# A two-layer graph transformer on one core: q of the second block, two row sums and the last feed-forward weights are placed elsewhere

## The chip, the core and the metric

The kernel runs on one core of one Trainium2 chip. The metric is the device time of one execution in microseconds (us), and the profile is one execution taken by the hardware profiler. Engines are named as in the profile: PE (matrix multiply), DVE (vector), ACT (scalar), POOL (GpSimd) and SP (the engine that only issues transfers here). ACT, SP and POOL each have a queue of their own for issuing DMA transfers. An instruction on an engine runs after the one ahead of it in that engine's order.

## The reference

Two layers of graph attention over N = 2708 nodes with 512 features, 8 heads of 64, and a feed-forward part of width 2048, all in float32. One layer, cut to what matters:

```python
mask = adj.astype(jnp.float32) + jnp.eye(n, dtype=jnp.float32)
q = (h @ Wq.T + bq).reshape(n, N_HEADS, D_K)
k = (h @ Wk.T + bk).reshape(n, N_HEADS, D_K)
v = (h @ Wv.T + bv).reshape(n, N_HEADS, D_K)
scores = jnp.einsum('nhd,mhd->hnm', q, k) / jnp.sqrt(jnp.float32(D_K))
scores = jnp.where(mask[None, :, :] == 0, jnp.float32(-1000000000.0), scores)
attn = jax.nn.softmax(scores, axis=-1)
ctx = jnp.einsum('hnm,mhd->nhd', attn, v).reshape(n, D_MODEL)
attn_out = ctx @ Wo.T + bo
h1 = _layer_norm(h + attn_out, ln1_g, ln1_b)
ff = jax.nn.relu(h1 @ W1.T + b1) @ W2.T + b2
h2 = _layer_norm(h1 + ff, ln2_g, ln2_b)
```

The adjacency matrix is sparse: a node has a handful of neighbours (22 at most are planned for), so attention only has to look at a short list for each node.

## The kernel before

**Lists and ranks.** `first` walks over the 22 tiles of 128 nodes (the last tile has 20) and makes k and v of layer 0 for each (line 835 and 841 on PE), which go to a table in memory, `kv_d`. Beside that, `lists` turns the rows of the adjacency matrix into lists of neighbours, `counted` counts them, and `ranked` (line 735) sorts all nodes by the length of their lists: two pairs of matmuls, a few DVE operations ending in `ranks` (line 764), 22 scatters by POOL to a table `rec_d` (line 768), and a load of the sorted lists back (line 779). From then on "tile g" means 128 nodes of the sorted order, tile 0 those with the longest lists and tile 21 the 20 with the shortest. `ident_i` (line 794) holds which node stands where, and a gather by it (`gather`, line 951) fetches rows of a table for one sorted tile. In layer 0, q and the rows of x are in the nodes' old order, so a sorted tile's q has to be gathered from `q_d`, and only after all of `q_d` has been written.

**Queries.** `first_queries` makes q of layer 0 for all 22 old tiles (t = 0 to 21, line 882), writing them to `q_d` in pairs through `written` (line 868). So that attention can begin ahead of the end of that, the q of some sorted tiles is made a second time from gathered rows of x: `own_rows` gathers x, `turned_own` transposes it on PE (tile `zT`, line 1100 and 1102), and `own_query` multiplies by Wq again (lines 922 and 923). At t = OWN = 9 this is done for the first block, tiles 21 and 20, whose q stays in a buffer; two steps on, for the second block, tiles 19 and 18, whose q goes out to a table `q_own` and comes back through SP when `asked` for it (line 971). `listed`, which turns the sorted lists into indices, stands at t = 8.

**Attention.** `attend` is a generator of steps. A step handles two list slots of one tile: POOL gathers the k and v rows of 128 neighbours for each slot (line 952, five `kv` buffers, asked for at least three chunks ahead), `weights` multiplies by q and sums over each head on DVE (lines 991 and 997), and a step later `weigh` takes exponents on ACT (line 1010), scales one slot's v on ACT (line 1017, eight operations) and the other on DVE (line 1023), and adds (line 1030). Two steps after a tile's last slot come `sums`, and three steps after it `divided`, which writes the finished tile `cx` on ACT (line 1061). The tiles are taken in the order 21, 20, 19, 18, 8, 9, 7, 10, ..., with planned list lengths (`CAPS`) of 3, 5, 6, 7, 10 and 9 slots for the first six. `advance` spends credit on steps and stops when two finished tiles wait; `through(k)` steps until block k is finished. The q of the next tile is asked for on the second step of a tile.

**Feed-forward.** The sorted tiles are taken in 11 blocks of two: (21, 20), (19, 18), (8, 9), ... `attended` transposes the block's `cx`, gathers x (`xb`), multiplies by Wo (`o`), adds and normalises (`h`; the square root of each normalisation is `rd` on POOL, line 1090). `turned` transposes `h` to `hT`. `feed_forward` runs 16 steps f: `pf` (line 1265, from `hT` and W1), `ft` on ACT (line 1273), and the products `a` with W2 three steps behind (line 1253). Within these steps `advance` puts attention of the next blocks: in block 0 with 1.1 credit up to f = 9, and at f = 10 the next block's `attended` begins.

**Weights.** W1 and W2 come in eight parts each (`load_w1`, `load_w2`), parts 0 and 1 during the last steps of `first`, parts 2 to 4 on ACT's queue during the first three steps of the queries, and parts 5 to 7 on SP's queue after all queries, since their places in memory hold the x and q tiles of the query stage until then. `load_second` (line 1137) loads rows of shift vectors and adds two pairs of them on DVE (`ln_b`, line 1144) inside `first`.

**Order.** PE, ACT and SP run in the order in which the program is written. DVE is so in the query stage, and POOL in `first` and `first_queries`; elsewhere the order on these two is set by a scheduler when the kernel is built, which may place an instruction of a later part ahead.

Of the kernel before, what the change touches and what calls it, by code (L numbers as in the profile page):

```python
# [18 lines left out]
P = 128  # L19
# [26 lines left out]
OWN = 9  # L46
# [424 lines left out]
def by_edges(ctx: ExitStack, tc: tile.TileContext, x, xT, adj, layers, out, good):  # L471
# [49 lines left out]
    q_own = dram.tile([N, DM], F32, name="q_own")  # L521
# [340 lines left out]
    def first_queries(bq, wq, listed, pa, tokens, meanwhile):  # L862
# [15 lines left out]
        for t in range(NT):  # L878
            r = size(t)
            if t % 2 == 0 and made:  # L880
                written()
            q = project(tokens(t, 1), r, wq, "q", other=t % 2 > 0)
            if t % 2 == 0:
                qs = wts.tile([P, 2, DM], F32, tag=f"w2_{5 + t // 2 % 3}", name="qs")
                made.append((t, qs))
            nc.vector.scalar_tensor_tensor(
                qs[:r, t % 2], q[:r], DK**-0.5, bq[:r], ALU.mult, ALU.add
            )
            if t == OWN - 1:
                listed()  # L890
                pa.__exit__(None, None, None)
                at = ctx.enter_context(tc.tile_pool(name="at", bufs=2))
                for g in blocks[0]:
                    own[g] = at.tile([P, DM], F32, tag="q", name="q", bufs=QB)
                to = dict(own)
                next(ahead)
            if t in (OWN, OWN + 2):
                k = (t - OWN) // 2
                zTs = [turned_own(g, xr) for g, xr in zip(blocks[k], xrs)]
                for g, xr, zT in zip(blocks[k], xrs, zTs):  # L900
                    own_query(g, zT, to.get(g, xr), bq, wq)
                    advance(0.5)
                xrs = [own_rows(g) for g in blocks[1]] if k == 0 else []
            meanwhile(t)
# [14 lines left out]
    def own_query(g, zT, to, bq, wq):  # L919

        r = size(g)
        q = project(lambda c: zT[:, c, :r], r, wq, "q")
        nc.vector.scalar_tensor_tensor(to[:r], q[:r], DK**-0.5, bq[:r], ALU.mult, ALU.add)
        if g in blocks[1]:
            nc.sync.dma_start(out=q_own[g * P : g * P + r, :], in_=to[:r])
# [35 lines left out]
    def asked(n, g):  # L961
# [5 lines left out]
        if n == 0 and g not in blocks[1]:  # L967
            gather(q[:r], q_d[0], ident_i[:r, g : g + 1])
        else:
            table = q_own if n == 0 else q_d[n]  # L970
            nc.sync.dma_start(out=q[:r], in_=table[g * P : g * P + r, :])
# [137 lines left out]
    class Layer:  # L1109
# [27 lines left out]
        def load_second(self, part, temp):  # L1137
# [3 lines left out]
            def sum_of(one, tag, other):  # L1141
                t, u = row(w, one, tag), temp()
                nc.sync.dma_start(out=u, in_=other.to_broadcast([P, DM]))
                nc.vector.tensor_tensor(t, t, u, ALU.add)
# [200 lines left out]
    def attend(n, got):  # L1345
# [15 lines left out]
        for k, step in enumerate(steps):  # L1361
            if step:
                g, s0, c, i, last = step
                if i == 0:
                    t = Tile(g, q)
# [3 lines left out]
                if i == 1 and g != order[-1]:  # L1369
                    q = asked(n, order[order.index(g) + 1])  # L1370
# [35 lines left out]
    early = {}  # L1406

    def beside_keys(t):
# [3 lines left out]
        if t > NT - 3:  # L1412
            now.load_second(t + 2 - NT, temp)
# [3 lines left out]
    def beside_queries(t):  # L1417

        if len(now.w2) < 5:
            now.load_w1(len(now.w1), nc.scalar)  # L1420
            now.load_w2(len(now.w2), nc.scalar)
        if t > OWN:
            advance(1.0 if t < NT - 7 else 0.45)
        if t == NT - 7:
# [3 lines left out]
        if t == NT - 6:  # L1428
# [10 lines left out]
    for j in range(len(now.w1), NFC // 2):  # L1439
        now.load_w1(j)  # L1440
        now.load_w2(j)
    behind, pool = None, []
    for n in range(NL):
# [26 lines left out]
        turning = projecting = None  # L1470
        for k, block in enumerate(blocks):
# [4 lines left out]
            for f, zs in enumerate(now.feed_forward(block, hs, hT)):  # L1476
# [8 lines left out]
                if more and f == 10:  # L1485
# [29 lines left out]
                if not last and not more:  # L1515
# [90 lines left out]
```

## Time and profile before

| what | value |
|---|---|
| time, median of 3 runs | 1980.74 us (1980.46 to 1982.29) |
| the profiled execution | 1984.12 us, of which the span of the trace is 1982.0 us |
| DVE busy | 1303.1 us (66%) |
| ACT busy | 934.6 us (47%) |
| POOL busy | 798.3 us (40%) |
| k and v stage ends, queries begin | 172.2 us |
| feed-forward of block 0 begins | 290.4 us |
| feed-forward of block 1 begins | 358.3 us |
| layer 1's first queries | about 1160 us |

Times within the trace are counted from the start of the span. An idle time of PE is shown with the instruction that released it, so that "PE waits for ft" means that PE's next multiply needed a tile that ACT wrote late. A line number belongs to the instruction, not to the place that called for it: all gathers by POOL are line 952, and only the tile's name tells which they are.

### The profile page before, as it was taken

What the parts mean: (1) busy time and instruction counts of PE and PEld (TensorE: products, weight loads), DVE (VectorE), ACT (ScalarE), POOL (GpSimd) and SP (SyncE); (2) the same over time, 40 slices, a digit from 0 to 9 for tenths busy, and PEclk for the clock granted to TensorE, in tenths of its full rate; (3) what the DMA queues carried; (4) which work ended last, traced back from release to release, by engine and by line L of the source; (5) the groups of instructions that cost most, each with busy time, mean ns of one, the idle gap of its engine ahead of it and who ended that gap; (6) DMA issues with size and microseconds to landing.
All of it is one profiled execution on the core that took longest, in us unless ns stands there. A gap on an engine that the chain in (4) does not pass through costs nothing. (4 is left out here: it accounts for less than half of the span.)

```text
span 1982.0 us, 20873 instructions
## 1 busy us (share of the span) xinstructions
PE 1903.5 (96%) x6162; PEld 1104.5 (56%) x6162; DVE 1303.1 (66%) x2140; ACT 934.6 (47%) x3219; POOL 798.3 (40%) x708
## 2 busy tenths in 40 slices
PE   8999888999999999999999997999999999999997
PEld 3443344565656556566566643556666566666664
DVE  6884478675957969568442025888587989777421
ACT  4660235464545646447441112665446765655320
POOL 3104436362634636435210023455356655544210
PEclk9999899999999999999999998999999999999998
DMA  8988658464745747455310746756465766554100
GB/s 321 357 296 293 191 200 296 154 208 143 227 154 174 236 150 246 154 173 176 133 58 22 225 157 225 258 182 212 155 208 186 244 205 225 177 188 151 42 11 13
DMA packets 131518, 367.96 MB, mean 186 GB/s; under 512 B 16701, under 2 KB 36525, under 8 KB 128687
## 3 DMA queue, kind: packets, MB, share of 16 engines
q0 software_dynamic: 69104, 246.35, 37.6%
q1 hardware_dynamic: 55780, 103.86, 15.3%
q10 hardware_dynamic: 6510, 16.34, 2.2%
q8 instruction: 50, 0.82, 0.2%
q14 instruction: 74, 0.60, 0.1%
HBM read 315.14 MB, written 51.35 MB: 185 GB/s over the span
## 5 line engine op out<-in xcount | busy, mean ns | idle before, releaser
L952 POOL DMA_INDIRECT kv<-kv_d,idx x420 | 547.0, 1302 | 494.0 <-DVE acc L1030 337.2
L1253 PE MATMUL a<-w,ft 128*128 128x512 f32 (+1 forms) x1408 | 665.3, 597 | 9.5 <-ACT ft L1273 9.5
L1265 PE MATMUL pf<-hT,w 128*128 128x256 f32 (+1 forms) x2816 | 638.2, 374 | 15.8 <-ACT ft L1273 8.0
L1265 PEld LDWEIGHTS pf<-hT,w 128*128 128x128 f32 x2816 | 523.2, 192 | 193.4 <-issue 107.7
L1253 PEld LDWEIGHTS a<-w,ft 128*128 128x128 f32 (+1 forms) x1408 | 255.9, 186 | 234.1 <-issue 198.3
L1273 ACT ACTIVATE ft<-pf,b 128x256 f32<-128x256 f32 (+1 forms) x352 | 157.9, 458 | 424.4 <-PE pf L1265 424.1
L991 DVE TENSOR_TENSOR kv<-kv,q 128x1024 f32<-128x1024 f32 (+3 forms) x222 | 256.5, 1158 | 144.6 <-DMA kv<-kv_d,idx 122.0
L1017 ACT ACTIVATE kv<-kv,p 128x64 f32<-128x64 f32 x1232 | 311.0, 335 | 5.0
L997 DVE TENSOR_REDUCE sc<-kv 128x16 f32<-128x1024 f32 (+3 forms) x222 | 254.6, 1153 | 1.0
L1030 DVE TENSOR_TENSOR acc<-acc,kv 128x1024 f32<-128x1024 f32 (+2 forms) x178 | 203.8, 1145 | 35.9 <-ACT kv L1017 35.4
L1090 POOL TENSOR_TENSOR rd<-va,mhalf 128x1 f32<-128x1 f32 (+1 forms) x88 | 85.7, 974 | 270.0 <-DVE va L1088 268.6
L1010 ACT ACTIVATE p<-sc,minus 128x8 f32<-128x8 f32 (+1 forms) x420 | 103.3, 295 | 190.3 <-DVE sc L997 189.9
L1023 DVE TENSOR_TENSOR kv<-kv,p 128x512 f32<-128x512 f32 (+1 forms) x178 | 121.5, 683 | 69.5 <-ACT p L1010 69.5
L568 PE MATMUL o<-wo,cT 128*128 128x512 f32 (+1 forms) x352 | 155.1, 593 | 0.5 <-ACT cT L1105 0.5
L568 PEld LDWEIGHTS o<-wo,cT 128*128 128x128 f32 (+1 forms) x352 | 65.1, 186 | 86.5 <-issue 75.8
L1061 ACT ACTIVATE cx<-acc,su 128x64 f32<-128x64 f32 (+1 forms) x352 | 88.5, 333 | 42.4 <-DVE su L1053 34.9
L1285 DVE TENSOR_TENSOR h<-a,h 128x512 f32<-128x512 f32 (+1 forms) x44 | 29.7, 677 | 106.0 <-PE a L1253 105.9
L1094 DVE SCALAR_TENSOR_TENSOR h<-h,rd,ln_b 128x512 f32<-128x512 f32 (+1 forms) x88 | 65.8, 748 | 48.1 <-POOL rd L1090 48.1
L660 ACT ACTIVATE code<-aj 128x2708 bf16<-128x2708 int32 (+1 forms) x22 | 73.3, 3330 | 48.1 <-POOL aj L656 41.2
L663 DVE MAX8 tops<-code 128x8 f32<-128x247 f32 (+2 forms) x242 | 82.8, 400 | 18.6 <-ACT code L660 18.5
L1017 ACT ACTIVATE acc<-kv,p 128x64 f32<-128x64 f32 (+1 forms) x352 | 88.8, 334 | 1.4
L568 PE MATMUL k<-wk,xg 128*128 128x512 f32 (+1 forms) x176 | 82.1, 611 | 6.8 <-DMA wk<-in_Wk 6.7
(132 smaller groups left out, 1466.3 us busy)
## 6 DMA issues: line engine op xcount, KB each, us to landing
aj<-in_adj SPq DMA_DIRECT2D x21, 1354.0 KB, 11.8
w<-in_W SPq DMA_DIRECT2D x26, 512.0 KB, 4.8
kv_d<-kvs ACTq DMA_DIRECT2D x21, 512.0 KB, 7.2
xg<-in_xT SPq DMA_DIRECT2D x20, 512.0 KB, 7.0
kv<-kv_d,idx POOLq DMA_INDIRECT x420, 5.6
q_d<-qs SPq DMA_DIRECT2D x22, 256.0 KB, 4.7
zT_d<-zT SPq DMA_DIRECT2D x22, 256.0 KB, 5.3
xb_d<-h SPq DMA_DIRECT2D x21, 256.0 KB, 5.3
```

Source lines behind the costliest of these rows:

```text
L568: nc.tensor.matmul(o[:r], xs(c), wm[:, c, :], start=(c == 0), stop=(c == NC - 1))
L952: nc.gpsimd.indirect_dma_start(out=to, out_offset=None, in_=table[:, :], in_offset=bass.IndirectOffsetOnAxis(ap=s, axis=0), bounds_check=N ...
L991: nc.vector.tensor_tensor(kv[:r, :c, :DM], kv[:r, :c, :DM], self.q[:r].unsqueeze(1).to_broadcast([r, c, DM]), ALU.mult,)
L997: nc.vector.tensor_reduce(self.sc[:r, s0 : s0 + c, :], kv[:r, :c, :DM].rearrange("p s (h d) -> p s h d", d=DK), AX.X, ALU.add,)
L1010: nc.scalar.activation(p[:r, s, :], self.sc[:r, s, :], AF.Exp, bias=minus[:r, g, s : s + 1])
L1017: nc.scalar.activation(to[:, i, hd], kv[:r, i, DM + h * DK : DM + (h + 1) * DK], AF.Copy, scale=p[:r, s0 + i, h : h + 1],)
L1023: nc.vector.tensor_tensor(to[:, 0, :].rearrange("p (h d) -> p h d", d=DK), kv[:r, 0, DM:].rearrange("p (h d) -> p h d", d=DK), p[:r, s0, : ...
L1030: nc.vector.tensor_tensor(self.acc[:r, :c, :], self.acc[:r, :c, :], kv[:r, :c, DM:], ALU.add)
L1061: nc.scalar.activation(cx[:r, hd], self.acc[:r, 0, hd], AF.Copy, scale=self.su[:r, h : h + 1])
L1253: nc.tensor.matmul(a[:r], fts[f][:, c0 : c0 + r], self.w2[f // 2][:, f % 2, :], start=(f == 0), stop=(f == NFC - 1),)
L1265: nc.tensor.matmul(pf[:, :w], self.w1[f // 2][:, c, f % 2 * P : f % 2 * P + P], hT[:, c, :w], start=(c == 0), stop=(c == NC - 1),)
L1273: nc.scalar.activation(ft[:, :w], pf[:, :w], AF.Relu, bias=self.b1[:, f : f + 1])
```

## The change

- OWN goes from 9 to 10. At t = 10 the q of block 0 (tiles 21 and 20) is made a second time, as before. The second making for block 1, the table `q_own` and its writes and reads are gone; tiles 19 and 18 gather q from `q_d` like all later tiles of layer 0. The q of tile 19 is not asked for ahead of its first step.
- In the queries, `advance(1.0)` is called for t = 11 to 15; block 0's `attended` begins at t = 16 and its `o` products come at t = 17 (15 and 16 before). No attention is stepped after that until the feed-forward of block 0.
- The two DVE additions of shift rows are kept in a list and made after t = 3 of the queries.
- Weight parts 5 to 7 are loaded from ACT's queue at f = 0, 2 and 4 of block 0's feed-forward of layer 0.
- During the feed-forward of block 0 in layer 0, POOL runs in program order.
- There, block 1's `attended` begins at f = 11 instead of 10, and its `o` at f = 12 instead of 11; credit of 1.1 lasts to f = 10.

```diff
-OWN = 9
+OWN = 10
...
-    q_own = dram.tile([N, DM], F32, name="q_own")
...
-            if t in (OWN, OWN + 2):
-                k = (t - OWN) // 2
-                zTs = [turned_own(g, xr) for g, xr in zip(blocks[k], xrs)]
-                for g, xr, zT in zip(blocks[k], xrs, zTs):
-                    own_query(g, zT, to.get(g, xr), bq, wq)
+            if t == OWN:
+                zTs = [turned_own(g, xr) for g, xr in zip(blocks[0], xrs)]
+                for g, zT in zip(blocks[0], zTs):
+                    own_query(g, zT, to[g], bq, wq)
                     advance(0.5)
-                xrs = [own_rows(g) for g in blocks[1]] if k == 0 else []
...
-        if g in blocks[1]:
-            nc.sync.dma_start(out=q_own[g * P : g * P + r, :], in_=to[:r])
...
-        if n == 0 and g not in blocks[1]:
-            gather(q[:r], q_d[0], ident_i[:r, g : g + 1])
-        else:
-            table = q_own if n == 0 else q_d[n]
-            nc.sync.dma_start(out=q[:r], in_=table[g * P : g * P + r, :])
+        fetch(n, q, q_d[n], g)
...
-                nc.vector.tensor_tensor(t, t, u, ALU.add)
+                if later is None:
+                    nc.vector.tensor_tensor(t, t, u, ALU.add)
+                else:
+                    later.append((t, u))
...
-                    t = Tile(g, q)
+                    t = Tile(g, q or asked(n, g))
+                    q = None
...
-                if i == 1 and g != order[-1]:
+                if i == 1 and g != order[-1] and (n > 0 or g != order[1]):
...
+        if t == 3:
+            for total, other in sums:
+                nc.vector.tensor_tensor(total, total, other, ALU.add)
...
-        if t > OWN:
-            advance(1.0 if t < NT - 7 else 0.45)
-        if t == NT - 7:
+        if OWN < t < NT - 6:
+            advance(1.0)
+        if t == NT - 6:
             through(0)
...
-        if t == NT - 6:
+        if t == NT - 5:
...
-    for j in range(len(now.w1), NFC // 2):
-        now.load_w1(j)
-        now.load_w2(j)
...
+        in_order = ExitStack()
+        if n == 0:
+            in_order.enter_context(tc.manual_schedule(engines={mybir.EngineType.Pool}))
...
-                if more and f == 10:
+                if more and f == 10 + (k + n == 0):
...
-                if more and f == 11:
+                if more and f == 11 + (k + n == 0):
...
-                advance(PACE[n] if k else 1.1 if f < 10 else 0.4)
+                advance(PACE[n] if k else 1.1 if f < 11 else 0.4)
...
+                if k == 0 and len(now.w1) < NFC // 2 and f % 2 == 0:
+                    now.load_w1(len(now.w1), nc.scalar)
+                    now.load_w2(len(now.w2), nc.scalar)
...
+            in_order.close()
```

More of the change, by code (lines that the diff above doesn't have):

```diff
@@ L1135, in load_w2, with load_second @@
             self.w2.append(t)
-        def load_second(self, part, temp):
+        def load_second(self, part, temp, later=None):
             w = self.w
@@ L1405, in by_edges @@
     ahead = attend(0, got)
-    early = {}
+    early, sums = {}, []
     def beside_keys(t):
@@ L1412, in beside_keys @@
         if t > NT - 3:
-            now.load_second(t + 2 - NT, temp)
+            now.load_second(t + 2 - NT, temp, sums)
             now.load_w1(t + 2 - NT)
```

## The prediction, made before the changed kernel ran

> **What bounds the kernel now.** I read the page first, then the share of PE in stretches of the trace, the waits of PE in the stretch that the change touches, and last the order of time of PE, DVE and ACT there.
>
> ```profile
> PE 1903.5 (96%) x6162; PEld 1104.5 (56%) x6162; DVE 1303.1 (66%) x2140; ACT 934.6 (47%) x3219; POOL 798.3 (40%) x708
> ```
>
> PE is busy for 96% of the span, so any multiply taken away, and any idle time of PE, is worth its full length, unless the idle time comes back later. In the stretches (length, then busy us of PE, PEld, DVE, ACT and POOL, granted clock) one sees where PE is not full:
>
> ```profile
> 172.20:206.70 34.50, 34.50 (x81) 15.08 (x80) 6.23 (x9) 0.58 (x1) 22.48 (x23) 1.00 0.82 265
> 206.70:226.20 19.50, 10.16 (x26) 3.76 (x26) 4.51 (x7) 0.94 (x3) 13.52 (x13) 0.74 0.68 218
> 226.20:290.40 64.20, 58.62 (x154) 24.69 (x152) 43.41 (x65) 23.23 (x94) 21.87 (x19) 0.99 0.57 191
> 290.40:358.30 67.90, 61.07 (x225) 33.01 (x226) 54.86 (x78) 36.21 (x142) 37.91 (x31) 0.94 0.81 286
> ```
>
> The four are the first ten q tiles, the wait for the ranks, the other queries, and the feed-forward of block 0. They hold 22 us of PE idle time; the next 800 us hold some 11. What PE waited for between 172 and 330 us (us in total, times, longest):
>
> ```profile
> PE tp L1100 <- DMA xr<-in_x,ident_i: 9.3, 2, 6.8
> PE pf L1265 <- ACT ft L1273: 6.8, 2, 4.8
> PE pf L1265 <- ACT hT L1105: 5.2, 1, 5.2
> ```
>
> And the places themselves, from the order of time:
>
> ```profile
> 172.16 34.60 PE L568 MATMUL q<-wq,xg 128*128 128x512 f32 x80
> 213.55 0.58 PE L1100 MATMUL tp<-ident,xr 20*128 20x20 f32 x4 [6.79 <-DMA xr<-in_x,ident_i]
> 216.68 1.09 PE L1100 MATMUL tp<-ident,xr 128*128 128x128 f32 x4 [2.55 <-DMA xr<-in_x,ident_i]
> ...
> 290.37 6.88 PE L1265 MATMUL pf<-hT,w 128*128 128x148 f32 x32 [5.21 <-ACT hT L1105]
> ```
>
> ```profile
> 168.11 0.69 DVE L1144 TENSOR_TENSOR ln_b<-ln_b,temp 128x512 f32<-128x512 f32 x1 [2.37 <-DMA temp<-in_bo]
> ...
> 307.34 1.22 DVE L991 TENSOR_TENSOR kv<-kv,q 128x1024 f32<-128x1024 f32 x1 [5.93 <-issue]
> ```
>
> ```profile
> 310.33 0.49 ACT L1010 ACTIVATE p<-sc,minus 128x8 f32<-128x8 f32 x2 [6.99 <-DVE sc L997]
> ...
> 317.54 2.02 ACT L1061 ACTIVATE cx<-acc,su 128x64 f32<-128x64 f32 x8
> ```
>
> The reader is to see three things. A q tile costs PE 34.60/10, or 3.43 us net of overlap. The row at 307.34 is tile 8, the first whose q comes from `q_d`: the last row of `q_d` left DVE at 294.9, so 12.5 us pass from there to the first use, with DVE blocked, ACT's exponents behind it, and `ft` behind those; that is PE's wait of 4.8. And the `cx` of tile 18 ends at 319.6, while PE asks for it only at 329.07 (the transposes of f = 10), so block 1's attention is now 9.5 us early.
>
> **The Trainium skill.** "TensorE: Matmul & The Clock Gate", What's actually happening, says that PE falls to half its clock after an idle window of about 3.4 us and needs as much busy time to recover. The trace agrees: after an idle time of 3.81 us at 647, eight `pf` take 3.62 us instead of 1.89, some 3.8 us lost in all; after 1.83 us at 513 nothing is lost. "DMA: Bandwidth & Descriptors", Issuing engines are not separate DMA queues, says that issuing from another engine only saves sequencer time; so moving weights to ACT's queue moves when they are issued, not what they take. Nothing else rests on a page.
>
> **The change part by part**, on the clock of the trace before.
>
> *Row sums.* The second addition held DVE until 168.7. The second pair of rank matmuls ends at 167.9, and then come 0.42, 0.43 and 0.18 us: ranks at about 169.1 instead of 170.6. POOL's 22 scatters (1.28 us apart), the load back, `ident_i` and the gathers of x follow 1.5 us earlier: x of tile 21 at 212.0, of tile 20 at 215.2. The two additions at t = 3 (1.4 us) lie in DVE's waits of 2.74 us per q and cost nothing; without that cover, 1.4.
>
> *OWN 10.* PE does an eleventh q, to 210.2, while it waits. Idle 1.9 and 2.6 instead of 9.3; with the earlier ranks PE is 1.5 + 3.4 = 4.9 us ahead.
>
> *Block 1's second q.* Eight transposes, their wait of 0.24 and 16 multiplies stood from 233.06 to 241.31: 8.2 us of PE gone. Also gone: two DVE operations (1.4), two gathers of POOL (2.6 with gaps), two copies on ACT, and four SP transfers. One of these came back 11.2 us after its issue and blocked DVE for 6.85 us, which delayed `hT`. POOL has two gathers of q more instead.
>
> *Attention of block 0.* PE reaches the transposes of `cx` after t = 16: 216.2 plus eight q of 3.43 plus about 0.9 of low clock is 244.6. DVE starts tile 21 at 220.8, idles until the q tile of t = 11 at 227.8, and then needs, from the rows before, 5.7 + 4.0 + 3.2 + 2.5 us for the steps of the two tiles and 0.65 for each of four q: 245.9, and `cx` by ACT at 248.2. So PE newly waits 3.6 us, and at that length loses some 2.6 to the clock. Bounds: 0 if the steps overlap better, 8 if slower. Then q of t = 17 (3.43), `o` (6.9), four q (13.7): the last q leaves PE at 275.7, DVE at 276.4. With DVE free, `hT` takes 2 us instead of 5.2: the feed-forward starts at 278.7, against 290.4.
>
> *Block 1's attention.* None of its 13 slots can start before its q is gathered. From 276.4: 3.2 us for the write (median of `q_d` here), 0.3, and 5.5 for the gather (median 5.6 for `kv`): 285.4. The other bound is the 12.5 seen, but with 3 MB of weights in flight, which now come later. From 285.4 DVE needs, at spacings of 1.13, 1.13, 0.60 and 1.13 us (L991, L997, L1023, L1030 near 310): 14.8 for the products, 9.3 for weighing, 2.2 for two `sums`, and 4.5 for two products of tile 8 that ACT's order puts ahead of `cx` 18: 30.8 us. ACT (2.5 for a chunk, 0.37 for `ft`, and six DMA issues of 0.5 to 1.5 us as at 173) keeps under the 4.0 of a DVE chunk but adds 1.3 at its tightest. Then ACT weighs a chunk, divides (2.0) and writes `ft` of f = 8: 322.1. PE, held by `ft` until there, does one `pf` and four `a` (3.2) and stands at the transposes of f = 11 at 325.3. Before, the same point of work is 329.07 + 3.03 = 332.1. So of 20 us (11.7, and PE's stalls of 8.3 with low clock) 6.8 are left.
>
> *One f later.* From `o` to the transposes of `h` PE has three f (9.1 us) instead of four. The norms of tile 18 ended 12.6 us after the first `o`; PE gets there 12.5 after it. Cost 0.4, bounds 0 and 3.
>
> *Weights on ACT.* Part 5 is issued near 291 and used at f = 10, past 315; hidden. Places: x and q tiles are done by then. Its cost is the issues counted above; if ACT's queue pushes back as SP's did (3.06 us for one issue at 298), 4 more.
>
> *POOL in order.* No `xb` of block 1 ahead of its turn: at 258 one blocked POOL for 17.4 us. In exchange a gather that waits for a buffer holds `rd` and q behind it. With five buffers and a lead of three, a gather goes out some 12 us before its use and lands in 5.6; cover 4 to 6 us. I take 0; bounds -1 and +6.
>
> Sum: -6.8 + 0.4 = -6.4 us. The profiled execution had 1984.12 (a span of 1982.0 and 2.1 around it), so 1977.7; it stood 3.4 above the median, so for the median 1974.3, which I round to 1974.5. Later blocks are filled by PE (791 of 802 us), so a lead is kept.
>
> **The rivals.** *PE sets the pace in block 0*: all 20 us stay, 1961. For it: DVE is idle before 276. Against: 30.8 us of DVE work behind a late q. *The gain is eaten*: q takes 11 us or the `cx` wait costs 4 more, and PE is where it was: 1979, within 0.2% (about 4 us, what a measurement of this kernel tells from no change). For it: the 12.5 us seen. *Slower*: POOL, in program order, lets gathers out only as buffers come free, and DVE waits in every chunk of block 1 and tile 8. Nine chunks at 5.4 us instead of 4.0 give +12.6, so +6: 1987. It decides from a spacing of 4.7. For it: DVE waited for `kv` up to 2.1 us in the stretch before; against: kv of tile 19 is loaded long ahead.
>
> **How the numbers follow.** Forecast 46%, its own range 1968 to 1977; all kept 6%; eaten 23%; slower 25%. Faster by over 0.2%: 0.52; within: 0.23; slower: 0.25. The best case of the terms (no `cx` wait, q in 8 us) is -15, the worst held -6.4 + 3.5 (q) + 4 (issues) + 4 (gathers) = +5. Range 1966 to 1986.
>
> **What would show it.** Right: first transposes of x near 212; `cx` waited for near 245; feed-forward from about 279; DVE's first product of tile 19 near 285; block 1's `pf` from about 352 (358.3 before). Wrong: q later than 289, a chunk above 4.7, or a new wait of PE after 360 of more than 4.

## The result and the profile after

| | before | after |
|---|---|---|
| time, median (least to most) | 1981.32 us (1980.46 to 1983.36) | 1993.0 us (1987.8 to 1997.39) |
| ratio to before, 95% interval | | 1.0054 [1.0035, 1.0074] |
| the profiled execution, its span | 1984.12, 1982.0 us | 1987.8, 1986.0 us |
| queries begin | 172.2 us | 167.5 us |
| feed-forward of block 0 begins | 290.4 us | 269.5 us |
| feed-forward of block 1 begins | 358.3 us | 360.8 us |
| feed-forward of block 2 begins | 439.0 us | 441.7 us |

The change makes the kernel slower by half a per cent. Its profiled execution was the fastest of its five, 5.2 us below their median, so the profile shows a part of the loss only. The table shows where that lies: block 0's feed-forward begins 20.8 us earlier (4.6 of them because the queries began earlier), block 1's 2.5 us later. All of the lead, and more, is lost inside one block's feed-forward, and the rest of the program runs as before (1543.0 us from block 2's feed-forward to the end before, 1544.3 after).

Work of PE fell as the change says. First the page's row of busy times, then the stretches (from and to, length, busy us of PE, PEld, DVE, ACT and POOL, granted clock, DMA share, GB/s) that correspond to the four shown of before:

```profile
PE 1902.5 (96%) x6138; PEld 1100.5 (55%) x6138; DVE 1302.3 (66%) x2138; ACT 932.2 (47%) x3217; POOL 798.5 (40%) x708
```

```profile
167.50:202.00 34.50, 34.50 (x82) 15.34 (x82) 7.42 (x11) 0.57 (x1) 22.33 (x23) 1.00 0.82 267
202.00:221.00 19.00, 15.62 (x37) 5.73 (x36) 6.01 (x9) 2.23 (x8) 10.42 (x11) 0.82 0.70 219
221.00:269.50 48.50, 46.48 (x118) 18.73 (x116) 29.45 (x49) 13.25 (x57) 11.63 (x10) 1.00 0.48 161
269.50:360.80 91.30, 67.55 (x224) 32.38 (x225) 64.07 (x85) 43.42 (x172) 46.20 (x41) 0.85 0.69 236
```

PE has 24 instructions fewer. The wait for the ranks costs 3.4 us of idle PE instead of 9.3, and the other queries are nearly full. The last stretch is the feed-forward of block 0: 91.3 us for 67.6 us of PE, where before it took 67.9 us for 61.1. Both idle time and low clock are there. What PE waited for from 230 to 365 us (us in total, times, longest):

```profile
PE pf L1259 <- ACT ft L1267: 20.0, 5, 8.2
PE tp L1091 <- DVE h L1085: 3.7, 1, 3.7
PE tp L1091 <- ACT cx L1052: 1.4, 3, 1.1
```

The places, from the order of time on PE. `tp<-ident,cx` are the transposes of block 1's finished attention, at f = 11:

```profile
269.54 4.31 PE L1259 MATMUL pf<-hT,w 128*128 128x148 f32 x32 [0.54 <-ACT hT L1096]
...
281.50 2.34 PE L1259 MATMUL pf<-hT,w 128*128 128x148 f32 x8 [5.62 <-ACT ft L1267]
...
308.95 1.27 PE L1259 MATMUL pf<-hT,w 128*128 128x148 f32 x8 [3.81 <-ACT ft L1267]
310.15 3.74 PE L1247 MATMUL a<-w,ft 128*20 128x512 f32 x4
...
322.12 2.34 PE L1259 MATMUL pf<-hT,w 128*128 128x148 f32 x8 [8.22 <-ACT ft L1267]
324.39 3.50 PE L1247 MATMUL a<-w,ft 128*20 128x512 f32 x4
327.72 1.04 PE L1091 MATMUL tp<-ident,cx 128*128 128x128 f32 x8
...
351.85 1.12 PE L1091 MATMUL tp<-ident,h 128*128 128x128 f32 x4 [3.68 <-DVE h L1085]
```

`ft` is written by ACT, which runs in program order behind the exponents of the attention, and these wait for DVE. So the next look is at DVE between 275 and 326:

```profile
285.60 2.36 DVE L982 TENSOR_TENSOR kv<-kv,q 128x1024 f32<-128x1024 f32 x2 [2.88 <-DMA q<-q_d,ident_i]
...
290.73 1.21 DVE L1021 TENSOR_TENSOR acc<-acc,kv 128x1024 f32<-128x1024 f32 x1
...
300.12 0.71 DVE L1014 TENSOR_TENSOR kv<-kv,p 128x512 f32<-128x512 f32 x1
303.57 1.23 DVE L982 TENSOR_TENSOR kv<-kv,q 128x1024 f32<-128x1024 f32 x1 [2.75 <-DMA q<-q_d,ident_i]
304.83 1.22 DVE L988 TENSOR_REDUCE sc<-kv 128x16 f32<-128x1024 f32 x1
305.97 1.22 DVE L1021 TENSOR_TENSOR acc<-acc,kv 128x1024 f32<-128x1024 f32 x1
307.10 1.22 DVE L982 TENSOR_TENSOR kv<-kv,q 128x1024 f32<-128x1024 f32 x1
...
314.70 1.23 DVE L982 TENSOR_TENSOR kv<-kv,q 128x1024 f32<-128x1024 f32 x1 [4.50 <-DMA kv<-kv_d,idx]
315.85 1.22 DVE L1021 TENSOR_TENSOR acc<-acc,kv 128x1024 f32<-128x1024 f32 x1
...
319.55 0.20 DVE L1044 RECIPROCAL su<-su 128x8 f32<-128x8 f32 x1
```

at one row of ACT, its half of a scaling:

```profile
292.95 2.02 ACT L1008 ACTIVATE kv<-kv,p 128x64 f32<-128x64 f32 x8
```

and at POOL, which issues the gathers:

```profile
282.73 0.99 POOL L947 DMA_INDIRECT kv<-kv_d,idx  x1 [0.30 <-issue]
292.21 1.20 POOL L947 DMA_INDIRECT kv<-kv_d,idx  x1 [8.50 <-DVE acc L1021]
...
297.12 1.38 POOL L947 DMA_INDIRECT q<-q_d,ident_i  x1 [0.30 <-issue]
...
307.45 1.73 POOL L947 DMA_INDIRECT kv<-kv_d,idx  x1 [5.07 <-DVE acc L1021]
...
317.33 1.20 POOL L947 DMA_INDIRECT kv<-kv_d,idx  x1 [6.86 <-DVE acc L1021]
```

Together they make a loop. A `kv` buffer is free when its chunk has been added (L1021). The addition at 305.97 had its operands at 300.83 (the scaling at 300.12, and ACT's half at 294.97), but on DVE it stood behind the product at 303.57, which waited for the q of tile 8. That q's gather had gone out only at 297.12, since POOL, in program order, had stood until 292.21 at a `kv` gather without a buffer. And because the addition ended late, POOL's next gather left at 307.45, its rows were not there at 310.20, and DVE waited 4.50 us for them, again with an addition behind. DVE's waits at 285.60, 296.94 (1.14, for a gather), 303.57 and 314.70 are 11.3 us together. PE adds 2.4: from `ft` to the transposes it needed 5.6 us instead of the 3.2 of full clock. DVE's own work up to the division (319.55) was 2.6 us more than predicted, 1.7 of it a third product and a first scaling of tile 8 that stand ahead of it, and ACT reached `ft` 2.4 us behind the division, where 5.9 had been reckoned. These four make the 12.7 us by which the stretch is longer than predicted (below).

The rows also show how far the additions lag. The chunks of tiles 19, 18 and 8 (3, 4 and 5 of them) are numbered through here; the first of a tile needs no addition. Chunk 5, tile 18's second, is added at 305.97, behind the product of chunk 8 (303.57), and chunk 6 at 315.85, behind that of chunk 10 (314.70). With five places, chunk 11 needs the place of chunk 6: its rows are asked for only when its product is already the next one. In the kernel before, each addition stood behind the product of the second chunk after its own.

### The profile page after: what moved, and what is told of

It reads as the page before. It is cut to its first block, busy times and chain, and to the rows that moved or that the text cites. A ratio compares the mean times of both kernels' runs of the same rounds, so it can differ in the third digit from the quotient of the medians.

```text
span 1986.0 us, 20810 instructions
## 1 busy us (share of the span) xinstructions
PE 1902.5 (96%) x6138; PEld 1100.5 (55%) x6138; DVE 1302.3 (66%) x2138; ACT 932.2 (47%) x3217; POOL 798.5 (40%) x708
## 5 line engine op out<-in xcount | busy, mean ns | idle before, releaser
L1021 DVE TENSOR_TENSOR acc<-acc,kv 128x1024 f32<-128x1024 f32 (+2 forms) x178 | 204.0, 1146 | 35.1 <-ACT kv L1008 34.6
L1279 DVE TENSOR_TENSOR h<-a,h 128x512 f32<-128x512 f32 (+1 forms) x44 | 29.9, 680 | 105.4 <-PE a L1247 105.3
L662 DVE MAX8 tops<-code 128x8 f32<-128x247 f32 (+2 forms) x242 | 82.9, 401 | 16.3 <-ACT code L659 16.2
L1318 POOL DMA_INDIRECT kv_d<-kvs,ident_i x22 | 22.7, 1031 | 164.9 <-ACT kvs L1312 89.6
```

The source lines that it names most:

```text
L1021: nc.vector.tensor_tensor(self.acc[:r, :c, :], self.acc[:r, :c, :], kv[:r, :c, DM:], ALU.add)
```

## The experiments

They were made one part at a time: first parts undone, then the two orders and the places of buffers, then combinations. "q to 1" is the time from the first query on PE to the feed-forward of block 1, "0 to 1" the part of it from the feed-forward of block 0 on, "1 to 2" the time from there to that of block 2, each from the one profiled execution (the start of the queries itself lies anywhere from 167.3 to 172.2 us in them). From the first query to block 0's feed-forward the changed kernel and the runs built on it took 97.0 to 102.7 us (e3 apart, 115.3), though no other edit touches that part; so what an edit does in block 0 is read from "0 to 1".

| run | ratio to before | q to 1 | 0 to 1 | 1 to 2 |
|---|---|---|---|---|
| before | | 186.1 | 67.9 | 80.7 |
| after | 1.0054 [1.0035, 1.0074] | 193.3 | 91.3 | 80.9 |
| e1 the same again | 1.0034 [1.0022, 1.0047] | 194.9 | 92.4 | 82.3 |
| e2 q one step sooner | 1.0021 [1.0012, 1.003] | 191.8 | 89.1 | 82.1 |
| e3 block 1's second q back | 1.0048 [1.0033, 1.0063] | 200.5 | 85.2 | 80.5 |
| e4 POOL free | 1.0012 [1.0001, 1.0024] | 185.8 | 88.7 | 81.1 |
| e5 two spare `kv` places | 0.9996 [0.9985, 1.0007] | 184.5 | 83.9 | 81.0 |
| e6 no credit after f = 11 | 1.0064 [1.0047, 1.0081] | 195.5 | 93.0 | 87.5 |
| e7 hand-over at f = 10 | 1.0007 [0.9995, 1.0019] | 186.0 | 85.0 | 82.4 |
| e8 row sums alone, on before | 1.0002 [0.9992, 1.0011] | 187.2 | 69.4 | 80.6 |
| e9 DVE in program order | 1.0001 [0.9991, 1.001] | 175.0 | 77.8 | 87.0 |
| e10 weights on SP | 0.9976 [0.9965, 0.9986] | 183.7 | 81.0 | 79.7 |
| e11 e2, e5 and e7 together | 0.996 [0.9948, 0.9973] | 172.6 | 75.6 | 82.9 |
| e12 e2, e5 and e9 together | 0.9991 [0.9982, 1.0] | 172.5 | 74.9 | 89.0 |
| e13 e9 and e10 together | 1.0005 [0.9996, 1.0014] | 178.4 | 78.5 | 88.9 |
| e14 e7 and e10 together | 0.9971 [0.9956, 0.9987] | 173.1 | 73.0 | 87.5 |
| e15 e2, e5, e7 and e10 together | 0.9975 [0.9965, 0.9986] | 175.4 | 73.2 | 88.6 |
| e16 e4 and e10 together | 0.9979 [0.9968, 0.999] | 184.9 | 82.2 | 79.9 |

**e1, the changed kernel once more**, unchanged.

> The changed kernel once more, unchanged, for its spread and a second trace. Its runs so far lay between 1987.8 and 1997.4 us, those of the kernel before within 3 us. Theory A (the loss is made in block 0's feed-forward, where gathers by POOL wait for one another): the spread comes from the same stretch, so a slower execution shows the additional time between 269 and 361 us of its trace. Theory B (the loss comes later, by chance): stretches after 361 us differ by several us between the two traces of this kernel.

It is slower than before again, with the same shape: a wait of 8.2 us ahead of the transposes of `cx`, and `h` waited for by 4.8. The cost is 0.3 to 0.5%. Of the 9.0 us by which this execution's span exceeds that of before, 5.6 had arisen by block 1's feed-forward and 3.4 came later. The 5.0 us between this span and that of the first profile are spread over the program, 1.9 ahead of block 0's feed-forward, 1.2 in it and 1.9 behind it, so neither theory has the spread. The same kernel gave 1.0054 and 1.0034: a difference of 0.002 between two runs is not read as anything by itself.

**e2, the q of tiles 18 and 8 asked for one step sooner**, on the first step of the tile ahead of each instead of the second.

```diff
                     q = None
+                    if n == 0 and g in order[2:4]:
+                        soon = order[order.index(g) + 1]
+                        own[soon] = asked(n, soon)
```

> The changed kernel, but the q of tile 18 is asked for right behind that of tile 19, and the q of tile 8 at the first step of tile 18, so that neither stands behind gathers of k and v that wait for a buffer. Theory A (q gathers late behind waiting gathers, POOL in program order): DVE's waits for q of tiles 18 and 8 (2.9 and 2.75 us) go, and the wait for k and v of 4.5 us behind them shrinks; block 1's transposes at about 319 instead of 327.7, the time 6 to 9 us below the changed kernel. Rival (the 4 us of DVE a chunk and ACT's queue set the pace): within 2 us of the changed kernel. Rival (five buffers set it): the waits for k and v grow by what the waits for q lose, within 3 us.

DVE's waits for q fall from 8.3 to 2.4 us between 262 and 330 us, and those for `kv` rise from 9.0 to 14.0. "0 to 1" fell by 2.2 us only: the loop holds with the buffers alone, as the last of the three expectations had it.

**e3, the second q of block 1 made again**, with `q_own` and its reads as before the change; all else of the change kept.

> The changed kernel with the second block's q made twice again (own rows gathered, transposed, multiplied, written to a table and read back through SP), everything else as changed; attention of block 1 still begins in block 0's feed-forward. Theory A (waiting for q from the full table costs block 0 its lead): the first product of tile 19 comes with the start of the feed-forward and q of 18 is there, so some 8 us of PE are added in the queries and more than that is won in block 0: 3 to 8 us below the changed kernel. Rival (DVE's work for 13 slots crowded into block 0 is what costs, whenever q is there): 5 to 8 us above the changed kernel, because the second q is paid for and nothing is won.

The ratio stays where it was, so neither forecast came true. The queries take 13.3 us longer, "0 to 1" is 6.1 us shorter, and "q to 1" grows by 7.2 (5.6 against e1). So leaving the second q out is no loss, and the late q of tile 19 is only a small part of what holds block 1: with it in hand, block 0 still takes 85.2 us instead of the 67.9 of before.

**e4, POOL free.**

```diff
-        if n == 0:
-            in_order.enter_context(tc.manual_schedule(engines={mybir.EngineType.Pool}))
```

> The changed kernel with POOL's order in block 0 left to the scheduler again. The order it gives has the three q gathers of tiles 19, 18 and 8 ahead of the gathers of k and v, but also puts x rows of block 1 ahead of the norms of block 0. Theory A (program order on POOL is what makes q late): as for the q asked for sooner, 4 to 9 us below the changed kernel, less what the early x rows block. Rival (program order is no loss): at or above the changed kernel by up to 10 us, with POOL blocked behind a gather of x rows and the norms of block 0 late.

The ratio falls by 0.002 against e1, and the two intervals just touch. "q to 1" is 7.5 us less, but 4.9 of that lie ahead of block 0's feed-forward, where the edit changes nothing; "0 to 1" falls by 2.6. The build gave DVE the same order here as in e2, up to the last division of tile 18, and "0 to 1" is the same as in e2 to 0.4 us: setting POOL free is worth what asking for q sooner is worth.

**e5, more places for k and v rows.** The ninth and tenth chunk of layer 0 (the first two of tile 18) use the places of Wk and Wv, which are idle then.

```diff
+            spare = {8: "wk", 9: "wv"}.get(count) if n == 0 else None
+            count += 1
+            if spare:
+                kv = wts.tile([P, SLOTS, 2 * DM], F32, tag=spare, name="kv")
+            else:
+                kv = at.tile([P, SLOTS, 2 * DM], F32, tag="kv", name="kv", bufs=KVB)
```

> The changed kernel with two more buffers for k and v in block 0: the first two chunks of tile 18 go to the places of the weights Wk and Wv, which are idle there, so that every later chunk waits for the release of the seventh before it instead of the fifth. POOL's order is the same. Theory A1 (five buffers set the spacing of chunks: a gather goes out only when DVE has weighed the chunk five before): DVE's waits for k and v between 280 and 328 us (about 9) and with them the late q of tile 8 go, block 1's transposes come 8 to 11 us earlier (near 318), the time 7 to 10 us below the changed kernel if the norms do not take it back. Theory A2 (only the q gathers are late): the waits for q stay, 2 to 4 us earlier. Rival (DVE's order, ACT behind it): within 2 us.

7.3 us of "0 to 1" come back, with every other part of the change in place; the additions stand as far behind the products as in the changed kernel, and only the waits are gone. Buffers that come free late are thus part of the cause. A wait of 6.7 us ahead of the transposes stays, and `h` is waited for by 3.9.

**e6, no credit from f = 11 on**, to see whether steps of tiles 8 and 9 stand in front of the normalisation.

```diff
-                advance(PACE[n] if k else 1.1 if f < 11 else 0.4)
+                advance(PACE[n] if k else 1.1 if f < 11 else 0.4 * n)
```

> The changed kernel without attention steps between f = 11 and f = 15 of block 0 in layer 0 (no credit is given there), so that DVE has only the norms of block 1 to do between the o products and the transposes of h. Theory B (one f less between o and the transposes of h, with attention of tile 8 in DVE's way, costs the 3.7 us wait and some 3 us of low clock after it): the wait of PE for h goes, from block 1's transposes to the start of its feed-forward 26 to 28 us instead of 33, the time 4 to 7 us below the changed kernel. Rival (the postponed steps come back): the wait goes, but block 1's or 2's own transposes then wait for cx by as much, within 2 us of the changed kernel. Rival (the wait comes from the late x rows or the root on POOL): the wait stays at 3 us or more.

The run doesn't decide this: credit left over still ran steps there, and the wait for `h` grew to 5.65 us. What was put off came up in the next block (87.5 us instead of 80.9).

**e7, block 1's hand-over at f = 10 and 11 again**, by the two conditions and the credit limit of before.

> The changed kernel with block 1's attended at f = 10 and o at f = 11 in block 0, as before the change. Theory B: four f between o and the transposes of h take away the wait of 3.7 us and the low clock behind it; PE stands at the transposes of cx 3 us of work sooner, while cx itself is as late as now (322 us), so PE waits there as long as it now waits for ft: 3 to 6 us below the changed kernel. Rival (cx decides, the place of the wait only moves): within 2 us.

PE now waits 6.7 us at the transposes of `cx`, but the wait for `h` is 1.2 us, and "0 to 1" is 6.3 us less. In the changed kernel the hand-over one f later costs by itself: the intervals of e7 and e1 are apart.

**e8, the row sums alone, put into the kernel before.**

> The kernel before with one part of the change: the two additions of shift rows are made after t = 3 of the queries instead of inside the keys stage. By the prediction's own step the ranks come 1.5 us earlier and the wait for the gathered x shrinks by as much. The trace of the changed kernel began its queries 4.6 us earlier and had its ranks 5.6 us earlier. Theory C (the additions held DVE while it waited for their rows, and the rank chain and PE behind it): queries begin at 167 to 169 us instead of 172, and 3 to 5 us are kept to the end. Rival (that difference is the arrival of adjacency rows, by chance): queries begin at 171 to 172, 0 to 2 us below the kernel before.

The ranks come 2.9 us ahead of the first query instead of 1.5, and the first transposes of x 41.3 us behind it instead of 41.4. No gain in the time can be measured.

**e9, DVE in program order beside POOL**, during the same feed-forward.

```diff
-            in_order.enter_context(tc.manual_schedule(engines={mybir.EngineType.Pool}))
+            in_order.enter_context(
+                tc.manual_schedule(engines={mybir.EngineType.Pool, mybir.EngineType.DVE})
+            )
```

> The changed kernel with DVE, too, in program order in block 0 of layer 0. The scheduler's order there puts the products of one or two later chunks, which wait for their k and v or q, ahead of the additions that release a buffer; program order has each chunk weighed right behind the next one's products. Theory A1' (the ring of five buffers and DVE's order together set the spacing: an addition stands behind a product that waits for a gather that waits for that addition's buffer): the release comes a chunk sooner, DVE's waits for k, v and q between 280 and 328 us (12 without the first) shrink to 6 or less, block 1's transposes come at 318 to 322 instead of 327.7, and the norms of block 1 are not broken up by products, so PE's wait for h falls below 2: the time 6 to 12 us below the changed kernel. Rival (DVE then waits for ACT's exponents and copies in every chunk): waits of 1 us a chunk take their place, within 3 us of the changed kernel. Rival (only the number of buffers matters): as the changed kernel.

The transposes of `cx` begin at 314.2 us, 41.3 us behind tile 19's first product (52.6 in the changed kernel), though weights, buffers and POOL are as they were. Each addition now stands behind one later product only, and "0 to 1" is 13.5 us less. PE's wait for `h` is 2.8 us, not below 2 as expected. The gain isn't kept: "1 to 2" is 6 us longer. The rows of PE and DVE show why:

```profile
337.48 0.66 PE L1091 MATMUL tp<-ident,h 128*128 128x128 f32 x4 [2.81 <-DVE h L1085]
...
357.92 2.07 PE L1247 MATMUL a<-w,ft 128*128 128x512 f32 x2 [4.87 <-DVE h L1279]
```

```profile
354.85 1.23 DVE L982 TENSOR_TENSOR kv<-kv,q 128x1024 f32<-128x1024 f32 x1 [0.61 <-issue]
356.53 0.74 DVE L1085 SCALAR_TENSOR_TENSOR h<-h,rd,ln_b 20x512 f32<-20x512 f32 x1 [0.45 <-POOL rd L1081]
357.19 0.67 DVE L1279 TENSOR_TENSOR h<-a,h 128x512 f32<-128x512 f32 x1
```

In program order DVE takes attention steps and one whole normalisation ahead of the addition that empties block 0's sums (L1279), and PE needs their place.

**e10, the last weights back on SP's queue, ahead of the feed-forward.**

```diff
+    for j in range(len(now.w1), NFC // 2):
+        now.load_w1(j)
+        now.load_w2(j)
...
-                if k == 0 and len(now.w1) < NFC // 2 and f % 2 == 0:
-                    now.load_w1(len(now.w1), nc.scalar)
-                    now.load_w2(len(now.w2), nc.scalar)
```

> The changed kernel with weight parts 5 to 7 on SP's queue behind the queries again. Theory (the weights on ACT are hidden, and keep 3 MB out of the way of the q and of the first gathers): with SP the first q of tile 19 lands 2 to 4 us later and all of block 0 follows, 2 to 4 us above the changed kernel. Rival (ACT's issues lie in the critical chain of exponents): 1 to 3 us below it. Rival (neither): within 1.

This alone turns the change into a gain, 0.9976, which none of the three forecasts had. The rows of DVE, with no wait shown between 280 and 319:

```profile
280.00 2.36 DVE L982 TENSOR_TENSOR kv<-kv,q 128x1024 f32<-128x1024 f32 x2 [10.73 <-DMA q<-q_d,ident_i]
...
288.12 1.22 DVE L982 TENSOR_TENSOR kv<-kv,q 128x1024 f32<-128x1024 f32 x1
289.26 1.22 DVE L1021 TENSOR_TENSOR acc<-acc,kv 128x1024 f32<-128x1024 f32 x1
290.39 1.21 DVE L988 TENSOR_REDUCE sc<-kv 128x16 f32<-128x1024 f32 x1
291.52 0.68 DVE L1014 TENSOR_TENSOR kv<-kv,p 128x512 f32<-128x512 f32 x1
292.12 1.22 DVE L982 TENSOR_TENSOR kv<-kv,q 128x1024 f32<-128x1024 f32 x1
293.26 1.22 DVE L1021 TENSOR_TENSOR acc<-acc,kv 128x1024 f32<-128x1024 f32 x1
...
312.60 0.20 DVE L1044 RECIPROCAL su<-su 128x8 f32<-128x8 f32 x1
```

With 3 MB of weights in flight the q of tile 19 comes later (DVE waits 10.7 us; in the changed kernel the product starts 6.3 us behind the last q). Yet from there the division of tile 18 ends in 32.8 us instead of 44.6, and the transposes of `cx` are reached in 38.3 instead of 52.6. What differs is the order in which DVE's instructions were built: each addition stands behind the product of the second chunk after its own, as in the kernel before, and never further back. That is so in all runs with these weights on SP's queue and DVE's order left to the build (before, e8, e10, e14, e15, e16); in all those with them on ACT's queue (after, e1 to e7, e11) one addition stands behind the product of the fourth.

**e11, three mends at once**: e2, e5 and e7 in one, with the weights left on ACT's queue and POOL in order.

> The changed kernel with three of the measured mends together: two more buffers in block 0, the q of tiles 18 and 8 asked for sooner, and block 1's attended at f = 10 again. If the causes are separate (gathers held by buffers, q behind them, one f too few for the norms), their gains add up: against the kernel before, the spare buffers alone gave 0.9996, f = 10 alone 1.0007, the changed kernel 1.0034 to 1.0054, so this gives 0.996 to 0.998. If they are one cause (all three only buy time for the same chain), it is no better than the best of them: 0.999 to 1.001.

1973.98 us median, 0.996 [0.9948, 0.9973]: faster than both kernels, so the gains add up. It has the lowest ratio here, but its interval overlaps those of e10, e14 and e15. What PE waits for from 230 to 365 us (lines stand five further on):

```profile
PE pf L1264 <- ACT ft L1272: 6.1, 2, 5.6
PE tp L1096 <- ACT cx L1052: 5.7, 2, 4.6
PE tp L1096 <- DVE h L1090: 1.6, 1, 1.6
```

13.4 us instead of 25.1. DVE's order still takes products ahead of additions, but with seven places that costs less.

**e12, e2 and e5 with DVE in program order.**

> The changed kernel with DVE in program order in block 0, two more buffers, and the q of tiles 18 and 8 asked for sooner. Theory A1': with the buffers and q's out of the way and DVE in order, a chunk takes the 4.0 us of DVE that the prediction had, block 1's transposes come near 315, and PE's wait for h is under 2: 0.994 to 0.997 of the kernel before. Rival (ACT sets the pace once DVE is in order: 2.5 us a chunk, ft and the wait of DVE for its copies): transposes near 320, 0.998 to 1.000.

Block 1 begins as early as in e11, and as in e9 it is lost behind it (PE waits 6.5 us for the addition that empties block 0's sums).

**e13, weights on SP and DVE in program order**: does the weights' queue cost by itself, or only by the order built beside it?

> Last weights of block 0 back on SP's queue before its feed-forward, and VectorE in program order there as GpSimd is. The theory 'VectorE's built order' says: what the weights on ScalarE's queue cost was the order of VectorE's instructions that the build made beside them. With the order given by hand, their place decides little: the transposes of tile 19's and 18's cx begin within 314 to 320 us whichever queue carries the weights (314.2 with them on ScalarE's), and the ratio is within 0.0015 of the 1.0001 that this order gave with the weights on ScalarE's queue. The rival 'the weights' transfers and issues on ScalarE's queue cost by themselves' says: taking them off gains again as much as it did alone, 0.006 of the time: a ratio of about 0.994 and transposes before 310.

With DVE's order given by hand, the queue of the weights makes no difference that is measured (1.0005 against 1.0001, intervals overlapping; "0 to 1" 78.5 and 77.8), where without it the same edit gave 0.006 to 0.008. Transposes at 321.2 are just outside the expected window, because this execution's queries began at 172.2; counted from there they come 149.0 us later, 144.1 in e9. So the rival, which wanted 0.994, falls.

**e14, weights on SP and the hand-over at f = 10.**

> Last weights of block 0 on SP's queue, and the hand-over of the keys back at f = 10 and 11. With the transposes ready at about 318 us the cx wait at f = 10 (which would stand near 322) is nothing, and the tail after it is shorter: the gains of the two edits alone (13.8 and 7 us against the changed kernel) are of different waits, so most of both should add: a ratio of 0.994 to 0.997. If the hand-over's gain was only of the late chunks that the other edit removes too, the ratio stays at 0.9976, that of the weights alone.

That the gains add isn't shown: 0.9971 can't be told from the 0.9976 of e10. "0 to 1" does fall by 8.0 us against e10, but "1 to 2" grows by 7.8, and the rows of PE, DVE and POOL behind the start of block 1 show one place:

```profile
377.61 4.64 PE L567 MATMUL v<-wv,zT 128*128 128x512 f32 x5 [4.95 <-DVE kvs L1310]
```

```profile
371.60 1.23 DVE L982 TENSOR_TENSOR kv<-kv,q 128x1024 f32<-128x1024 f32 x1 [6.28 <-DMA kv<-kv_d,idx]
...
376.88 1.27 DVE L1310 TENSOR_TENSOR kvs<-k,bk 20x512 f32<-20x512 f32 x2
```

```profile
359.84 4.30 POOL L947 DMA_INDIRECT xb<-in_x,ident_i  x1 [0.30 <-issue]
364.44 1.41 POOL L947 DMA_INDIRECT kv<-kv_d,idx  x1 [0.30 <-DVE sc L988]
```

POOL took 4.3 us over a gather of x, the rows behind it came late, and DVE stood 6.3 us at their product, with the k of layer 1 (L1310) behind it; PE needs the place of that k. Why that gather took so long is not shown.

**e15, e14 with the spare places and the sooner q.**

> The same two edits together with two spare places for k and v rows and the last queries asked for one tile sooner. If the loop of five buffers still holds VectorE with the weights on SP's queue, 3 to 6 us less than the two edits give: a ratio of 0.992 to 0.994. If the order that the build makes beside the weights on SP's queue already frees every buffer in time, no more than the two edits give (within 0.001).

No more than e14: where DVE's order frees each buffer in time, further places are worth nothing that is measured. PE waits 5.7 us at the same place.

**e16, weights on SP and POOL free**: is POOL's program order a cost of its own?

> Weights on SP's queue and GpSimd free of program order: of the change only the single q, the row sums and the hand-over one f later are left. If GpSimd's program order is a cost of its own (with the weights on ScalarE's queue its removal gave 0.004 of the time), the ratio falls from the 0.9976 of the weights alone to 0.994 or 0.995. If it cost only by standing behind VectorE's built order, which is good here, the ratio stays within 0.0015 of 0.9976, or rises, since gathers of x and q are built ahead of their turn as before the change.

0.9979 against 0.9976. No cost is measured here; POOL's order cost something, some 0.002 (e4 against e1), only while it stood behind DVE's late additions.

## Why the prediction was wrong

From the first query to block 1's feed-forward the prediction had 179.8 us (172.2 to 352); the profile has 193.3. By its steps:

| step | predicted | measured | off by |
|---|---|---|---|
| first query to feed-forward of block 0 | 106.5 | 102.0 | -4.5 |
| to tile 19's first product | 6.7 | 5.6 | -1.1 |
| to the transposes of `cx` | 39.9 | 52.6 | +12.7 |
| to the feed-forward of block 1 | 26.7 | 33.1 | +6.4 |

- *Row sums*: the ranks came 0.8 and 1.3 us earlier against the first query (here and in e8), where 1.5 was predicted, but the first transposes of x only 0.5 and 0.1 us earlier; nothing of it can be measured in the time (e8).
- *OWN 10* held: 3.4 us of idle PE at x, where 4.5 were reckoned. *Block 1's second q* held: 24 PE instructions are gone, and e3 puts the second q at 5.6 to 7.2 us.
- *Attention of block 0*: too dear. The wait for `cx` is 1.4 us in all and not 3.6, and the clock stays at 1.00.
- ***Block 1's attention*, the step that failed.** The product's start, counted from the feed-forward, was right to 1.1 us. The 30.8 us for DVE were a sum of its spacings in the trace before, and took for granted that DVE never waits once q is there. From the first product of tile 19 to the last division of tile 18 DVE took 44.6 us, 11.3 of them waits; e10, with the same products ahead of the division and no waits, takes 32.8. So the sum of work was short by 2 us, further steps of tile 8; the larger error is the waits, put at nothing. By the prediction's count of nine chunks the 44.6 us are 5.0 each, past the point of decision of 4.7 (its own sum gives 3.4 by this count). The rival "slower" had the size: 12.6 us of waiting, a ratio of 1.003, where 1.0054 and 1.0034 were measured. That its 1987 is so near the profiled execution's 1987.8 is luck, since that was the fastest of five. And its reason, POOL's program order with few buffers, holds only behind the order that DVE was given here: with that of e10 neither is measured to cost anything (e16, e15).
- *POOL in order*, taken at 0 with a bound of +6, and *Weights on ACT*, taken as hidden: no cost of either by itself is measured (e16, e13), and so neither price can be put beside the other. The weights' move changes the order that is built for DVE, with additions behind products that wait (after against e10); that order makes buffers come free late (e5 mends it by more places, e9 by another order); and in POOL's program order the next q's gather stands behind the one that has no buffer (e2 and e4 take that away, for 2.2 and 2.6 us). The prediction listed only the issues on ACT for the weights. It gave every instruction of DVE the order of the trace before, though that order is made anew at each build.
- *One f later*, taken at 0.4 with a bound of 3, is the second term that failed: 6.4 us. The 12.6 us from `o` to the norms were read where DVE had few steps between. In the changed kernel products, scalings and additions of tiles 8 and 9 stand between the additions and the norm, and PE waits 3.7 us and loses clock. e7 confirms it: 6.3 us back.
- *The range* ended at 1986, below the rival's 1987, to which it gave 25%: its sum of the worst left out the bounds that the prediction itself names for the wait for `cx` and for the hand-over, and two of the six us for POOL.

The prediction's main reason, that PE has 8 us less to do, was right, and its size comes near where DVE's additions stand as they did before: e10, the change without its new queue for the weights, is at 0.9976, where the forecast stood for 0.997, and e16, without POOL's order too, at 0.9979. The 0.996 of e11 shows that more can be kept with both placements left in, but only with places and a hand-over that the change didn't have. Why the build orders DVE differently with the weights on ACT's queue is not shown by any run. Nor is it shown why the median of the change's executions lies 5 us above the profiled one.

## What to carry to other kernels

Where the order of an engine is made at build time, an edit on another engine's queue can change it: a duration taken from the trace of before may hold where a spacing doesn't. Look for additions (or whatever frees a buffer) that are ordered behind an instruction that waits for a load, because then the wait comes back as the next load's lateness, and count how many later chunks stand ahead of the one that frees: here, with five places, two left little or no waiting and up to four left 11 us of it. More buffers, or an order that frees first, break the loop. And judge a gain at the start of a block only together with the next block: e9, e12 and e14 took 13 to 18 us less than the changed kernel from block 0's feed-forward to block 1's, and then 6 to 8 us more to block 2's.

## What the runs showed of the hardware

- The granted clock after idle time, in the changed kernel: after 5.62 and 8.22 us eight `pf` took 2.34 us instead of 1.17. After 3.81 us the `pf` still had full speed (1.27), and the four `a` behind them took 3.74 instead of 2.09. The Trainium skill, "TensorE: Matmul & The Clock Gate", What's actually happening, gives an idle window of about 3.4 us and calls it free-running. In these traces shorter waits cost too, which that figure does not cover. In e9 eight `pf` took 2.34 us after 3.27, and twelve `a` 7.22 behind a wait of 2.81; in e12 twelve `a` took 5.52 behind a wait of 2.83. So near 3 us the length of a wait alone does not tell whether it costs clock. The rows, first of e9, then of e12:

```profile
305.38 2.34 PE L1259 MATMUL pf<-hT,w 128*128 128x148 f32 x8 [3.27 <-ACT ft L1267]
...
338.06 7.22 PE L1247 MATMUL a<-w,ft 128*20 128x512 f32 x12
```

```profile
337.87 0.66 PE L1096 MATMUL tp<-ident,h 128*128 128x128 f32 x4 [2.83 <-DVE h L1090]
338.46 5.52 PE L1252 MATMUL a<-w,ft 128*20 128x512 f32 x12
```

- The first product with a gathered q started 6.3 us behind the last q on DVE in the changed kernel, where ACT issued the first of the weights only after it, and 10.7 us behind it with 3 MB of them issued on SP's queue just before (e10). In the other runs (e3 apart, whose q was made earlier) the two placements gave 5.9 to 6.4 and 9.6 to 10.7. So issuing them later did help the gather, by some 4 us, though the kernel lost more elsewhere.
